# Cross-attention on one core: column parts of 171 in place of 172, another order of work in the first rounds, and two moved shifts in the tail

## The chip, the core and the metric

The kernel runs on one core of a Trainium2 chip. The core has a matrix engine (PE in the profile, with PEld for its weight loads), a vector engine (DVE), a scalar engine (ACT), GpSimd (POOL), and SP, which here only issues DMA transfers. Each engine executes its own list of instructions in order and waits on semaphores for the others. The metric is device time of one execution in microseconds (us), the median of several runs.

## What is computed

Per batch element b (64 of them), with x of 256 x 512 and a context c of 256 x 384, all in fp32:

```python
text_p  = x @ W_text + b_text            # 256 x 512
audio_p = c @ W_audio + b_audio          # 256 x 512
Q = layer_norm(text_p, g1, beta1)
K = layer_norm(audio_p, g2, beta2)
alpha = softmax(Q @ K.T / sqrt(512))     # 256 x 256
h = (alpha @ audio_p) @ W_out + b_out
out = layer_norm(h + x, g_out, beta_out)
```

## The kernel before

**Algebra.** The weights are centred once, so that the layer norms of Q and K need only a mean square. `alpha @ audio_p @ W_out` is computed as `(alpha @ c) @ (W_audio W_out)`; the folded matrix is `wao_sb` (384 x 512), made by `fold_multiply` and `fold_evict` (lines 237 to 249). Two of the three matrix products of a round are done with fewer multiplications than the direct way:

- `Fork` (from line 609), for x times W_text: sums of blocks, seven products in place of eight, on columns of 256. It lives in two PSUM banks, `fork`, with parts R, q1, q2 and q3. `seed` puts a bias row into R, `clear` zeroes q2, then `one`, `seven`, `six`, `five` and `rest` multiply, with `after_one` (copy R to q1, ACT), `after_seven` (copy q2 out, ACT), `after_six` and `after_five` (DVE) between them.
- `Thirds` (from line 502), for c times W_audio (object `k2` of a round) and for z times wao (`old.o`): the 384 inner columns and the 512 output columns are cut in three, 15 products in place of 18. `W3` (line 50) is the width of a column part, 172; the parts start at columns 0, 172 and 340 (`starts`), so that the middle and the last one overlap by four columns. They live in four PSUM banks, `third`, two parts each (M, L, TU, N). `one` to `five` multiply, `after_one`, `after_three` and `after_four` (DVE) combine parts in PSUM between them, `after_five` and `leave`, or `leave_plus` for the output, take the result to rows. `ends(row)` is the first and last part of a row, `middle(row)` the middle one; `room` is a buffer of one or two parts.

Both need sums of blocks of the moving side: `sum_x` (line 289, four additions, on GpSimd except the first) and `Sides` (line 305, seven additions on GpSimd). `third_weights` (line 343) makes the sums of weight parts once, in groups of instructions numbered 0, 3, 1 and 2.

**Order.** `manual_schedule`: each engine executes its instructions in the order of the program text; every line of the main part is therefore a choice of order for each engine that it uses. After the head (lines 975 to 1084) comes the loop `for b in range(B - 2)` (line 1093). Round b multiplies the projections of batch b+2 (`k2`, `q2`), turns the rows of Q and K of batch b+1 (`turn`, a 32 x 32 transposition on DVE of blocks that were stored to DRAM and fetched again by `store` and `fetch`), applies gamma and beta to those of batch b (`affine_keys`, `affine_queries`, ACT), computes the scores of batch b (`at.score`), its maxima (DVE) and exponentials (ACT), the context of batch b-1 (`last.context_one`, `context_two`), and the output of batch b-2 (`old.o`). `settled` is batch b-3, whose final layer norm is done by `shift` (DVE), `scale_row` (ACT) and `lift_rows` (GpSimd), or `settle` (one DVE instruction for the last two of these). Rounds 0, 1 and 2 differ from the others by `if b` cases, because old and last do not exist yet, and because the folded weights are still being made. All DMAs of the loop are issued by SP, in program order: `load_c` and `load_x` (four transfers each), `store`, `fetch`, `store_e`, `fetch_e`.

The tail from line 1295 finishes the last four batches without projections.

Of the kernel before, what the change touches and what calls it, by code (L numbers as in the profile page):

```python
# [9 lines left out]
F32 = mybir.dt.float32  # L10
# [12 lines left out]
def kernel(  # L23
# [25 lines left out]
    scale = 1.0 / math.sqrt(H)  # L49
    W3 = -(-H // 12) * 4  # L50
    starts = (0, W3, H - W3)
# [236 lines left out]

    def sum_x(xT, engine=nc.gpsimd):

        n = DC // 2
        part = lambda i, j: xT[:, j * n : (j + 1) * n, bass.ts(i, P)]
        s = work.tile([P, 4, n, P], F32, tag="xsum", name="xsum")
        add = engine.tensor_tensor
        add(s[:, 0], part(1, 0), part(1, 1), ALU.add)
        add(s[:, 1], s[:, 0], part(0, 0), ALU.subtract)
        add(s[:, 2], part(0, 0), part(1, 0), ALU.subtract)
        add(s[:, 3], part(0, 1), s[:, 1], ALU.subtract)
        ss = {
            1: part(0, 0), 2: part(0, 1), 4: part(1, 1),  # L300
            5: s[:, 0], 6: s[:, 1], 7: s[:, 2], 3: s[:, 3],
        }
        return {p: [ap[:, k, :] for k in range(n)] for p, ap in ss.items()}

    class Sides:
# [37 lines left out]
    def third_weights(w_sb, t, parts=(0, 1), engine=nc.gpsimd):  # L343

        b = [[w_sb[:, c, j : j + W3] for j in starts] for c in range(3)]
        w = {n: t[:, i] for i, n in enumerate((10, 4, 5, 1, 6, 2, 8, 9, 0, 3, 7))}
        w.update({14: b[2][0], 13: b[1][2], 11: b[0][0], 12: b[0][2]})
        plus = lambda o, i0, i1: engine.tensor_tensor(o, i0, i1, ALU.add)
        less = lambda o, i0, i1: engine.tensor_tensor(o, i0, i1, ALU.subtract)
        if 0 in parts:  # L350
            plus(w[0], b[1][1], b[1][2])
            less(w[6], w[0], b[2][0])
            less(w[2], b[1][0], w[0])
            plus(w[0], b[0][0], b[1][0])
            less(w[8], w[2], w[0])
        if 3 in parts:
            plus(w[0], w[0], b[1][2])
            less(w[9], b[1][2], b[2][0])
            less(w[7], b[0][1], b[0][0])
            plus(w[7], w[7], b[0][2])  # L360
        if 1 in parts:
            less(w[3], b[2][1], b[2][0])
            less(w[10], w[3], b[0][2])
            plus(w[4], w[3], b[2][2])
# [137 lines left out]
    class Thirds(Projection):  # L502

        M, L, TU, N = [t[:, : 2 * W3].rearrange("p (n h) -> p n h", n=2) for t in third]
        M0, M1, L0, L1 = M[:, 0], M[:, 1], L[:, 0], L[:, 1]
# [41 lines left out]
        def room(self, tag, n=1):  # L547
            return once.tile([P, n, W3] if n > 1 else [P, W3], F32, tag=tag, name=tag)

# [501 lines left out]
    wa_t = const.tile([P, 11, W3], F32, tag="wa_thirds", name="wa_thirds")  # L1051
# [13 lines left out]
    fold_evict(1)  # L1065
    cT[2] = turn_c(2)
    cs[2] = Sides(cT.pop(2), "csum").add()
    q[1].five()
# [15 lines left out]
    wao_t = wao_room[:, : 11 * W3].rearrange("p (n h) -> p n h", n=11)  # L1084

# [7 lines left out]
    for b in range(B - 2):  # L1093
# [17 lines left out]
        k2.one()  # L1111
        k2.after_one()
        if b < 2:
            Fork.clear()
        if b == 0:
            bias_rest(part, 3, 4)
        if b == 1:
            last.maxima()
        k2.two()
        if old:  # L1120
            old.context_two(0)
            old.context_two(1)
            old.copy_two()
        k2.three()
        if b == 0:
            fold_multiply(2, 2, 4)
            fold_evict(2)
            fold_bias(part)
        if three and b > 1:
            cT[b + 3] = turn_c(b + 3)  # L1130
        if b > 1:
            at.affine_keys(0, 1)
        k2.after_three()
        if b < 2:
            cT[b + 3] = turn_c(b + 3)
        if old:
            old.start_products()
        if b < 3:
            q2.one()
            q2.after_one()  # L1140
        q2.seven()
        q2.after_seven()
        if b > 1:
# [5 lines left out]
        done = settled  # L1149
        if b > 1:  # L1150
            last.fetch_e()
            load_c_rows(b)
            load_x_rows(b - 1)
# [5 lines left out]
        if b == 1:  # L1159
            last.reciprocals()  # L1160
            last.divide_e()
            last.store_e()
            load_c(b + 4)
            last.fetch_e()
            load_c_rows(b)
            load_x(b + 4)
        if b < 2:
            at.q.turn()
            at.k.turn()
            at.affine_keys()  # L1170
        if settled:
            settled.deviations()
        if three:
            cs[b + 3] = Sides(cT.pop(b + 3), "csum").add(2 if b > 1 else 7)
        k2.four()
# [12 lines left out]
        k2.leave()  # L1188
        k2.last_middle()
        if three:  # L1190
            cs[b + 3].add(3 if b > 1 else 0)
        if old:
# [8 lines left out]
        q2.scales()  # L1201
        if b:
            q[b + 1].turn()
            k[b + 1].turn([0])
        if three:
            xT[b + 3] = turn_x(b + 3)
        k2.square()
        if b:
            k2.scales()
            at.score(0, 2)  # L1210
        else:
            at.score(0, 8)
            xs[b + 3] = sum_x(xT.pop(b + 3))
            k2.scales()
        if old:
            old.o.one()
            old.o.after_one()
            old.o.two()
        if b:
            k[b + 1].turn([1])  # L1220
            at.score(2, 4)
# [19 lines left out]
        if old:  # L1241
            old.o.five()
        if three:
            Fork.seed()
            k2.normalise()
            k2.store()
            q2.fetch()
            k2.fetch()
        if three:
# [7 lines left out]
        if b < 2:  # L1257
            wao_blocks = third_weights(wao_sb, wao_t, [[0, 3], [1, 2]][b])
        if b:
            at.maxima()  # L1260
        if three and b:
            Fork.clear()
        if b:
            at.exponentials()
# [44 lines left out]
    settled.shift(0)  # L1309
    settled.shift(1)  # L1310
    old.o.two()
# [3 lines left out]
    old.o.three()  # L1315
    old.o.after_three()
    for t in range(ST):
        last.context_two(t)
# [109 lines left out]
```

## Time and profile before

| | |
|---|---|
| median of 3 runs | 1381.71 us (1380.88 to 1382.01) |
| the profiled execution | 1381.61 us |
| its span, first to last instruction | 1379.8 us |
| mean granted clock of PE in it | 0.999 |
| busy: PE, PEld | 1363.6 us (99%), 1242.3 us (90%) |
| busy: DVE, ACT, POOL | 1102.3 (80%), 1090.2 (79%), 1160.3 us (84%) |
| DMA | 322.02 MB, mean 233 GB/s |

A row of a timeline reads: start in us from the span's start, length in us, engine, line, operation, what it writes `<-` what it reads, partitions x elements, and, in square brackets, how long the engine had been idle before and what ended that. Neighbouring rows of the same kind are merged, with their count after `x`. A row of a group reads: line, engine, operation, tiles, shapes, `x` count, busy us, mean ns of one, idle us before them. Each product of two fp32 matrices appears as two MATMUL records, and the records of consecutive ones overlap: what a product costs is the distance from start to start.

### The profile page before, as it was taken

To read this page: it belongs to the slowest core of one execution; us is meant where nothing else is said; L and a number is where in the kernel's file an instruction comes from. 1 tells how busy PE (TensorE), PEld (TensorE's weight loads), DVE (VectorE), ACT (ScalarE), POOL (GpSimd) and SP (SyncE) were. 2 spreads that over 40 slices of the span, in tenths; PEclk is the share of its full clock that TensorE was granted. 3 is DMA by queue.
4 is the path that set the end of the run, shared out by engine and by line. 5 is a ranking of instruction groups with operands and counts; after the bars stand their busy time and mean duration, and the time that the engine had idled before them with its cause. 6 is when DMAs were issued, how large, how long until landed. Compare 5 with 4: busy or idle time off the path is not lost.

```text
span 1379.8 us, 26390 instructions
## 1 busy us (share of the span) xinstructions
PE 1363.6 (99%) x7423; PEld 1242.3 (90%) x7423; DVE 1102.3 (80%) x2689; ACT 1090.2 (79%) x2688; POOL 1160.3 (84%) x1927
## 2 busy tenths in 40 slices
PE   9899999999999999999999999999999999999997
PEld 4689999999999999999999999999999999999995
DVE  6668888888888878888888888888887888888768
ACT  4578888787887887887888888888888888887884
POOL 5687888888888888888888888888888888888866
PEclk9999999999999999999999999999999999999999
DMA  9599778778788889787888788897888887888673
GB/s 214 161 256 241 241 234 242 230 245 249 234 235 253 232 235 244 232 249 236 244 243 243 238 241 236 238 236 243 246 241 242 236 250 232 237 246 237 206 223 112
DMA packets 449096, 322.02 MB, mean 233 GB/s; under 512 B 153781, under 2 KB 381621, under 8 KB 448950
## 3 DMA queue, kind: packets, MB, share of 16 engines
q1 hardware_dynamic: 448854, 320.20, 80.7%
q8 instruction: 60, 0.98, 0.3%
q14 instruction: 86, 0.70, 0.2%
q10 hardware_dynamic: 96, 0.13, 0.0%
HBM read 203.57 MB, written 116.65 MB: 232 GB/s over the span
## 4 chain that ended last, share of the span: by engine, by line
PE 92%; DVE 2%; DMA 2%; POOL 1%; ACT 1%; issue 1%; SPq 0%; DVEq 0%; POOLq 0%; ACTq 0%
PE ps_f L629 26%; PE ps_m L516 15%; PE ps_sc L697 15%; PE ps_z L763 12%; PE ps_n L516 10%; PE ps_u L516 8%; PE ps_l L516 5%; DMA wt<-in_L_xattn_W_text_dram 1%; POOL csum L327 1%; DMA wo<-in_L_xattn_W_out_dram 1%; DMA c<-in_ctx_dram 0%; ACT qT L491 0%; DMA kd<-kr 0%; PE ps_m L843 0%; DMA cq<-in_ctx_dram 0%
## 5 line engine op out<-in xcount | busy, mean ns | idle before, releaser
L697 PE MATMUL ps_sc<-kT,qT 128*128 128x256 f32 x1024 | 261.5, 379 | 0.0
L327 POOL TENSOR_TENSOR zsum<-zsum,zT 128x256 f32<-128x256 f32 x305 | 193.7, 652 | 14.3
L697 PEld LDWEIGHTS ps_sc<-kT,qT 128*128 128x128 f32 x1024 | 186.2, 190 | 18.2 <-ACT qT L491 1.2
L629 PE MATMUL ps_f<-wtsum,xsum 128*128 128x256 f32 x756 | 184.6, 380 | 2.8 <-ACT ps_f L640 1.6
L763 PE MATMUL ps_z<-eT,c 128*128 128x256 f32 x768 | 186.4, 379 | 0.4 <-ACT e L714 0.3
L327 POOL TENSOR_TENSOR csum<-csum,cT 128x256 f32<-128x256 f32 x310 | 174.4, 571 | 10.0
L763 PEld LDWEIGHTS ps_z<-eT,c 128*128 128x128 f32 x768 | 143.0, 190 | 18.0 <-ACT e L714 0.5
L951 POOL TENSOR_TENSOR yr<-yr,beo 128x512 f32<-128x512 f32 x122 | 153.5, 1280 | 3.6 <-ACT yr L947 3.6
L629 PEld LDWEIGHTS ps_f<-wtsum,xsum 128*128 128x128 f32 x756 | 138.0, 190 | 18.1 <-ACT ps_f L640 2.3
L327 POOL TENSOR_TENSOR zsum<-zT 128x256 f32<-128x256 f32 x122 | 72.4, 593 | 95.3 <-ACT zT L781 95.3
L390 POOL TENSOR_TENSOR rstd<-ve,nhalf 128x2 f32<-128x2 f32 x192 | 136.3, 710 | 16.0
L491 ACT ACTIVATE kT<-kT,columns 128x256 f32<-128x256 f32 x256 | 139.5, 596 | 6.0 <-DVE kT L484 5.1
L491 ACT ACTIVATE qT<-qT,columns 128x256 f32<-128x256 f32 x256 | 139.1, 593 | 2.8 <-DVE qT L75 2.8
L629 PE MATMUL ps_f<-wt,xT 128*128 128x256 f32 x504 | 129.3, 379 | 0.0
L714 ACT ACTIVATE e<-ps_sc,nmx 128x256 f32<-128x256 f32 x128 | 59.5, 470 | 66.5 <-DVE nmx L707 66.5
L933 DVE SCALAR_TENSOR_TENSOR yr<-yr,nm,go 128x512 f32<-128x512 f32 x124 | 103.0, 831 | 0.9 <-ACT junk L826 0.9
L629 PEld LDWEIGHTS ps_f<-wt,xT 128*128 128x128 f32 x504 | 93.1, 190 | 10.7 <-issue 0.7
L500 DVE TENSOR_TENSOR ps_l<-ps_m,t 128x172 f32<-128x172 f32 x248 | 85.8, 346 | 18.3 <-DVE t L557 1.8
L500 DVE TENSOR_TENSOR ps_f<-ps_f,s 128x256 f32<-128x256 f32 x126 | 54.5, 433 | 47.1 <-PE ps_f L629 42.0
L781 ACT COPY zT<-ps_z 128x256 f32<-128x256 f32 x64 | 23.9, 373 | 86.3 <-PE ps_z L763 86.2
L826 ACT ACTIVATE junk<-yr,nm 128x512 f32<-128x512 f32 x124 | 88.0, 713 | 2.8 <-POOL nm L807 2.8
L947 ACT ACTIVATE yr<-yr,rstd 128x512 f32<-128x512 f32 x122 | 87.2, 716 | 1.2 <-POOL rstd L390 1.1
(247 smaller groups left out, 3785.4 us busy)
## 6 DMA issues: line engine op xcount, KB each, us to landing
kd<-kr SPq DMA_DIRECT2D x64, 512.0 KB, 3.1
kq<-kd SPq DMA_DIRECT2D x256, 128.0 KB, 3.1
qd<-qr SPq DMA_DIRECT2D x64, 512.0 KB, 2.8
qq<-qd SPq DMA_DIRECT2D x256, 128.0 KB, 2.7
xq<-in_x_dram SPq DMA_DIRECT2D x252, 128.0 KB, 3.2
x<-in_x_dram SPq DMA_DIRECT2D x63, 512.0 KB, 4.6
out_dram<-yr SPq DMA_DIRECT2D x62, 512.0 KB, 3.9
cq<-in_ctx_dram SPq DMA_DIRECT2D x252, 96.0 KB, 3.2
```

What stands on the lines that cost most here:

```text
L327: nc.gpsimd.tensor_tensor(*step)
L390: nc.gpsimd.tensor_tensor(r, ve, nhalf[:, :n], ALU.pow)
L491: nc.scalar.activation(self.T[:, k, :], self.T[:, k, :], AF.Identity, bias=bet[:, k : k + 1], scale=gam[:, k : k + 1],)
L500: nc.vector.tensor_tensor(o, i0, i1, op)
L516: nc.tensor.matmul(place, lhsT=self.sides.of[n], rhs=self.weights[n], start=(n == 14), stop=True, skip_group_check=True,)
L629: nc.tensor.matmul(place, lhsT=side, rhs=w, start=False, stop=True, skip_group_check=True)
L697: nc.tensor.matmul(self.sc[:, t, :], lhsT=self.q.T[:, k, bass.ts(t, P)], rhs=self.k.T[:, k, :], start=(k == 0), stop=(k == HC - 1),)
L763: nc.tensor.matmul(ps, lhsT=c_rows[self.b][:, s, bass.ts(j, P)], rhs=self.eT[:, s, :], start=(s == 0), stop=(s == ST - 1),)
L826: nc.scalar.activation(junk, self.y[:, t, :], AF.Square, bias=self.nm[:, t : t + 1], accum_out=self.ssq[:, t : t + 1],)
L933: nc.vector.scalar_tensor_tensor(row, row, self.nm[:, t : t + 1], go_sb, ALU.add, ALU.mult)
L947: nc.scalar.mul(self.y[:, t, :], self.y[:, t, :], self.r[t])
L951: nc.gpsimd.tensor_tensor(self.y[:, t, :], self.y[:, t, :], beo_sb, ALU.add)
```

## The change

1. `W3` becomes 171 (`-(-H // 3)`), the parts start at columns 0, 171 and 341 and overlap by one column. Buffers and PSUM parts keep a pitch of `WP` = 172.
2. In the head: `take_columns` (a PE transposition that waits for small vectors from DRAM) stands behind `fold_multiply(0)`; the four additions of the first `sum_x` are spread, s[:, 2] for product 7 first; `turn_c(2)` and its `Sides`, the third group of weight sums, `Thirds.seed_with` and `ba_delta` stand elsewhere. All calls of `sum_x` now do s[:, 2] first.
3. In rounds 0 to 2: other places for `turn`, `affine_keys`, `exponentials`, `divide_e`, `fold_multiply(2, 2, 4)`, `k[2].fetch` and `fetch_e`; in round 1 product `one` of the fork stands before `k2.three`. A group of `third_weights`, [1], is split in [1] and [4].
4. In the tail: `settled.shift(1)` behind `old.o.after_three`, `old.shift(0)` behind `last.o.after_four`; for the last batch, row tile 0 is finished by `scale_row` and `lift_rows` in place of `settle`, and stored last.

No instruction is added to the rounds from 3 on, and none taken away. The diff, cut to its core (the class `SumX` holds the additions of `sum_x` as a list, of which `add(n)` emits the next n):

```diff
-    W3 = -(-H // 12) * 4
+    W3 = -(-H // 3)
+    WP = -(-W3 // 4) * 4
...
-        M, L, TU, N = [t[:, : 2 * W3].rearrange("p (n h) -> p n h", n=2) for t in third]
+        M, L, TU, N = [t[:, : 2 * WP].rearrange("p (n h) -> p n h", n=2)[:, :, :W3] for t in third]
...
-    g1_sb, be1_sb, g2_sb, be2_sb, bac_sb = take_columns()
     turn_weights(2, 2)
...
     xT[1] = turn_x(1)
+    xs_1 = SumX(xT.pop(1), nc.vector)
+    xs_1.add(1)
     k[1].evict(0)
     k[1].evict(1)
     Fork.clear()
+    xs_1.add(2)
...
-    xs[1] = sum_x(xT.pop(1), nc.vector)
-    for v in (g2_sb, be2_sb):
-        nc.vector.tensor_scalar(v, v, scale, None, ALU.mult)
+    xs[1] = xs_1.add()
+    cT[2] = turn_c(2)
...
     k[1].square()
-    ba_delta = third_bias(ba_sb, "ba_delta")
     fold_multiply(0)
+    g1_sb, be1_sb, g2_sb, be2_sb, bac_sb = take_columns()
+    for v in (g2_sb, be2_sb):
+        nc.vector.tensor_scalar(v, v, scale, None, ALU.mult)
...
-    third_weights(wa_sb, wa_t, [1, 2], nc.vector)
+    cs[2] = Sides(cT.pop(2), "csum").add()
+    ba_delta = third_bias(ba_sb, "ba_delta")
+    third_weights(wa_sb, wa_t, [1], nc.vector)
     fold_multiply(1, 0, 2)
     q[1].six()
     q[1].after_six()
+    third_weights(wa_sb, wa_t, [4, 2], nc.vector)
     fold_evict(0)
+    Thirds.seed_with(ba_sb)
...
-    cT[2] = turn_c(2)
-    cs[2] = Sides(cT.pop(2), "csum").add()
     q[1].five()
     q[1].after_five()
     xT[2] = turn_x(2)
...
-    Thirds.seed_with(ba_sb)
...
+            if b == 2:
+                last.fetch_e()
...
         k2.after_one()
+        if b == 0:
+            bias_rest(part, 3, 4)
+            at.q.turn()
         if b < 2:
             Fork.clear()
-        if b == 0:
-            bias_rest(part, 3, 4)
...
         k2.two()
+        if b == 0:
+            fold_multiply(2, 2, 4)
+            fold_evict(2)
+        if b == 1:
+            q2.one()
+            q2.after_one()
...
         k2.three()
         if b == 0:
-            fold_multiply(2, 2, 4)
-            fold_evict(2)
             fold_bias(part)
...
+        if b == 1:
+            last.exponentials()
...
         k2.after_three()
+        if b == 1:
+            last.reciprocals()
         if b < 2:
             cT[b + 3] = turn_c(b + 3)
+        if b == 0:
+            at.k.turn()
...
         q2.after_seven()
-        if b > 1:
+        if b == 1:
+            last.divide_e()
+        if b < 3:
+            at.affine_keys()
+        else:
             at.affine_keys(2, 3)
-        if b == 1:
-            last.exponentials()
...
         if b == 1:
-            last.reciprocals()
-            last.divide_e()
             last.store_e()
+            k[2].fetch()
+            last.fetch_e()
...
-        if b < 2:
-            at.q.turn()
-            at.k.turn()
-            at.affine_keys()
...
-        if b:
-            q[b + 1].turn()
-            k[b + 1].turn([0])
+        q[b + 1].turn()
+        k[b + 1].turn([0])
...
         k2.square()
+        k2.scales()
...
             at.score(0, 8)
             xs[b + 3] = sum_x(xT.pop(b + 3))
-            k2.scales()
...
+        if b == 1:
+            at.maxima()
+            at.exponentials()
...
     settled.shift(0)
-    settled.shift(1)
...
     old.o.after_three()
+    settled.shift(1)
...
     at.shift(0)
-    old.shift(0)
     end.maxima()
     end.exponentials()
     last.o.four()
     last.o.after_four()
+    old.shift(0)
...
     end.evict_halves(1, [0])
+    end.shift(0)
+    end.scale_row(0)
     end.evict_halves(1, [1])
     end.scale_soon(1)
+    end.lift_rows(0, 1)
     end.shift(1)
-    end.shift(0)
-    end.settle(0)
+    end.settle_halves(1)
     end.store(0, 1)
-    end.settle_halves(1)
```

More of the change, by code (lines that the diff above doesn't have):

```diff
@@ L287, in weight_sums, with __init__, add, sum_x @@
         return {p: [ap[:, k, :] for k in range(n)] for p, ap in ws.items()}
[L289 to L303, printed above, removed]
+    class SumX:
+        def __init__(self, xT, engine=nc.gpsimd):
+            n = DC // 2
+            part = lambda i, j: xT[:, j * n : (j + 1) * n, bass.ts(i, P)]
+            s = work.tile([P, 4, n, P], F32, tag="xsum", name="xsum")
+            self.engine = engine
+            self.steps = [
+                (s[:, 2], part(0, 0), part(1, 0), ALU.subtract),
+                (s[:, 0], part(1, 0), part(1, 1), ALU.add),
+                (s[:, 1], s[:, 0], part(0, 0), ALU.subtract),
+                (s[:, 3], part(0, 1), s[:, 1], ALU.subtract),
+            ]
+            ss = {
+                1: part(0, 0), 2: part(0, 1), 4: part(1, 1),
+                5: s[:, 0], 6: s[:, 1], 7: s[:, 2], 3: s[:, 3],
+            }
+            self.of = {p: [ap[:, k, :] for k in range(n)] for p, ap in ss.items()}
+        def add(self, n=4):
+            for step in self.steps[:n]:
+                self.engine.tensor_tensor(*step)
+            self.steps = self.steps[n:]
+            return self.of
+    def sum_x(xT):
+        return SumX(xT).add()
     class Sides:
@@ L345, in third_weights @@
         b = [[w_sb[:, c, j : j + W3] for j in starts] for c in range(3)]
-        w = {n: t[:, i] for i, n in enumerate((10, 4, 5, 1, 6, 2, 8, 9, 0, 3, 7))}
+        w = {n: t[:, i, :W3] for i, n in enumerate((10, 4, 5, 1, 6, 2, 8, 9, 0, 3, 7))}
         w.update({14: b[2][0], 13: b[1][2], 11: b[0][0], 12: b[0][2]})
@@ L363, in third_weights @@
             less(w[10], w[3], b[0][2])
+        if 4 in parts:
             plus(w[4], w[3], b[2][2])
@@ L547, in room @@
         def room(self, tag, n=1):
-            return once.tile([P, n, W3] if n > 1 else [P, W3], F32, tag=tag, name=tag)
+            room = once.tile([P, n, WP] if n > 1 else [P, WP], F32, tag=tag, name=tag)
+            return room[:, :, :W3] if n > 1 else room[:, :W3]
         def after_one(self):
@@ L1050 @@
     q[1].after_seven()
-    wa_t = const.tile([P, 11, W3], F32, tag="wa_thirds", name="wa_thirds")
+    wa_t = const.tile([P, 11, WP], F32, tag="wa_thirds", name="wa_thirds")
     third_weights(wa_sb, wa_t, [0])
@@ L1149 @@
         done = settled
+        if b > 2:
+            last.fetch_e()
         if b > 1:
-            last.fetch_e()
             load_c_rows(b)
@@ L1173 @@
         if three:
-            cs[b + 3] = Sides(cT.pop(b + 3), "csum").add(2 if b > 1 else 7)
+            cs[b + 3] = Sides(cT.pop(b + 3), "csum").add(2 if b else 7)
         k2.four()
@@ L1189 @@
         k2.last_middle()
+        if b == 0:
+            third_weights(wao_sb, wao_t, [1])
         if three:
-            cs[b + 3].add(3 if b > 1 else 0)
+            cs[b + 3].add(3 if b else 0)
         if old:
@@ L1218 @@
             old.o.two()
+        k[b + 1].turn([1])
         if b:
-            k[b + 1].turn([1])
             at.score(2, 4)
@@ L1247 @@
             q2.fetch()
-            k2.fetch()
+            if b:
+                k2.fetch()
         if three:
@@ L1262 @@
             Fork.clear()
-        if b:
+        if b > 1:
             at.exponentials()
```

13 lines of the change are left out of this document (6 added, 7 removed).

## The prediction

> **What bounds the kernel now.** First the page, for the engine that is never idle, then the table by stages.
>
> ```profile
> span 1379.8 us, 26390 instructions
> ...
> PE 1363.6 (99%) x7423; PEld 1242.3 (90%) x7423; DVE 1102.3 (80%) x2689; ACT 1090.2 (79%) x2688; POOL 1160.3 (84%) x1927
> ```
>
> ```profile
> 26.00:106.00 80.00, 73.64 (x343) 58.06 (x344) 52.98 (x115) 52.80 (x130) 61.72 (x109) 1.00 0.78 213
> 106.00:1333.00 1227.00, 1226.90 (x6827) 1140.59 (x6826) 1000.21 (x2462) 1001.39 (x2473) 1060.10 (x1759) 1.00 0.83 240
> 1333.00:1372.00 39.00, 38.73 (x185) 30.79 (x184) 30.83 (x79) 24.64 (x60) 26.28 (x37) 1.00 0.38 122
> 1372.00:1379.80 7.80, 0.23 (x2) 0.00 (x0) 4.13 (x9) 0.09 (x1) 1.72 (x3) 0.74 0.37 134
> ```
>
> The columns are length, then busy time of PE, PEld, DVE, ACT and POOL. From 106 us to 1333 us PE is busy 1226.90 of 1227 us: there only shorter matmuls save time, and the other engines matter only if they come to hold PE up. From 26 to 106 us (the end of the head, and rounds 0 to 2) PE is idle by the record for 6.4 us; behind the last matmul follow 7.6 us of vector work and stores. The timeline of PE shows all waits of that second stage that it counts as idle:
>
> ```profile
> 26.06 0.30 PE L169 MATMUL ps_v<-ident,vectors 128*128 128x128 f32 x1 [0.40 <-DMA vectors<-in_L_xattn_b_audio_dram]
> ...
> 32.73 1.10 PE L629 MATMUL ps_f<-wtsum,xsum 128*128 128x256 f32 x4 [1.25 <-POOL ve L388]
> ...
> 44.52 0.85 PE L516 MATMUL ps_m<-wa,csum 128*128 128x172 f32 x4 [0.54 <-ACT ps_m L530]
> ...
> 47.65 1.10 PE L254 MATMUL ps_bias<-part,ones 128*128 128x512 f32 x2 [0.27 <-DVE part L228]
> ...
> 55.19 0.85 PE L516 MATMUL ps_m<-wa_thirds,cT 128*128 128x172 f32 x4 [0.95 <-DVE ps_u L500]
> ...
> 64.17 0.53 PE L516 MATMUL ps_u<-wa_thirds,csum 128*128 128x172 f32 x2 [0.32 <-DVE ps_u L500]
> ...
> 67.98 1.13 PE L629 MATMUL ps_f<-wtsum,xsum 128*128 128x256 f32 x4 [1.55 <-ACT ps_f L640]
> ...
> 73.03 0.85 PE L516 MATMUL ps_m<-wa_thirds,cT 128*128 128x172 f32 x4 [1.01 <-DVE ps_u L500]
> ...
> 84.09 1.13 PE L763 MATMUL ps_z<-eT,c 128*128 128x256 f32 x4 [0.27 <-ACT e L714]
> ```
>
> These nine add up to 6.6 us. Each costs more than its bracket, because records overlap: the next product should have started about 0.16 us before the previous record ended, and the second record of a product comes about 0.1 us late. So a bracket plus 0.26 is its price, 8.9 us for the nine; with waits too short to leave PE idle I put this pool at about 10 us. The change can win there, in the column width, and in the tail.
>
> **The columns.** What a column costs:
>
> ```profile
> L516 PE MATMUL ps_n<-wa,csum 128*128 128x172 f32 x248 | 46.4, 309 | 0.0
> L763 PE MATMUL ps_z<-eT,c 128*128 128x256 f32 x768 | 186.4, 379 | 0.4 <-ACT e L714 0.3
> L843 PE MATMUL ps_f<-wao,zT 128*128 128x512 f32 x12 | 5.5, 592 | 0.0
> ```
>
> ```profile
> 0.00:1379.80 1379.80, 625.59 (x3720) 585.62 (x3720) 1.00 0.81 233
> ```
>
> A record of 172 columns lasts 309 ns, of 256 columns 379, of 512 columns 592: (379 - 309) / 84 = 0.83 ns a column, and (592 - 379) / 256 = 0.83 again. The second row counts the records of line 516, all of 172 columns: 3720. One column less on each, on an engine that does not stop, is 3720 x 0.83 = **3.1 us**. No row has an odd width or an odd first column (172, 256, 512; starts 0, 172, 340). The bounds are 3.1 us saved, if the line holds, and nothing saved, if an odd width is handled like the next even one; a loss by odd widths has no row either way, and stands as a rival below. I take 3.1, since three widths lie on one line.
>
> **The head, to 40.6 us.** The wait at 26.06 goes: the transposition for the vectors now stands behind eight records of folded products, and its DMA has landed by then.
>
> ```profile
> 27.01 3.60 PE L240 MATMUL ps_m<-wo,waT 128*128 128x512 f32 x8
> ```
>
> They take 3.60 us less the overlap of 0.16, so 3.4, and four of them 1.7. Going earlier only brings PE sooner to the next wait, at 32.73, for product 7. It needs a cleared q2 and the sum s[:, 2], which DVE made third:
>
> ```profile
> 28.51 1.29 DVE L415 TENSOR_TENSOR kr<-ps_f,ba 128x512 f32<-128x512 f32 x2 [1.59 <-DMA kd<-kr]
> 29.93 0.27 DVE L625 MEMSET ps_f<- 128x256 f32 x1
> ...
> 31.81 0.77 DVE L297 TENSOR_TENSOR xsum<-xT 128x256 f32<-128x256 f32 x1
> ...
> 32.98 0.33 DVE L349 TENSOR_TENSOR wa_thirds<-wa 128x172 f32<-128x172 f32 x1
> ...
> 33.60 0.68 DVE L348 TENSOR_TENSOR wa_thirds<-wa_thirds,wa 128x172 f32<-128x172 f32 x1
> ...
> 40.64 1.03 PE L629 MATMUL ps_f<-wt,xsum 128*128 128x256 f32 x4
> ```
>
> Now s[:, 2] fits into the 1.59 us in which DVE waits for a store to land. The memset still ends at 30.2, because that landing is not moved, so product 7 can start at about 30.7, when PE has done the folded products: 2.0 us sooner. Each product of the fork is 1.03 less 0.16, so 0.87 us (last row). Product 7, four folded records and product 6 bring PE to 34.2. But this is partly given back. Seven sums of weight parts ([4, 2]) now stand between `after_six` and `after_five`. Alone one takes 0.33 us, beside GpSimd 0.68, and GpSimd is adding there too (the sums of `cs[2]`, which the change brings forward). `after_six` and the first two weight sums end by about 35.4; seven more take 2.3 to 4.8 us, so `after_five` (some 0.4) ends between 38.1 and 40.6. The products of `rest`, which stood at 40.64, start then, or at 38.5, where PE itself is ready (34.2 + 1.7 + 0.87 + 1.7). The gain at this point is 0 to 2.0 us; I take **0.6**, near the contended end.
>
> **Rounds 0 to 2.** In the order of the rows above:
> - 44.52: the seed of M is copied long before. Bracket plus 0.26: 0.8.
> - 47.65: the bias sum now precedes other DVE work, and 1.7 us of folded products stand between `two` and `three`, which cover `after_one`. 0.5.
> - 55.19: DVE turned Q and K ahead of `after_four`:
>
> ```profile
> 53.27 1.26 DVE L484 STREAM_TRANSPOSE kT<-kq 128x512 f32<-128x512 f32 x2
> 54.46 0.30 DVE L500 TENSOR_TENSOR m<-ps_m,ba_delta 128x172 f32<-128x172 f32 x1
> ```
>
> The turns move ahead of `after_six`, and so the wait of 1.2 goes, but `after_six` now has the turn of K (1.26) and a turn of c before it, so product `five` will wait some 0.4. Net 0.8. ACT also gets gamma and beta done earlier, which takes away two short waits among the scores: 0.3.
> - 64.17: `three` waits for `after_one`, which is two DVE instructions:
>
> ```profile
> 63.31 0.34 DVE L552 COPY n<-ps_n 128x172 f32<-128x172 f32 x1 [3.46 <-PE ps_n L516]
> 63.68 0.35 DVE L500 TENSOR_TENSOR ps_u<-ps_n,n 128x172 f32<-128x172 f32 x1
> ```
>
> `q2.one`, 0.87 us of matmuls, now stands in between and covers them. 0.6.
> - 67.98: the copy of R to q1 stood on ACT behind the scaling of K's rows:
>
> ```profile
> 66.33 1.33 ACT L452 ACTIVATE kr<-kr,rstd 128x512 f32<-128x512 f32 x2 [2.30 <-POOL rstd L390]
> ```
>
> The copy came right behind it. ACT waited 2.30 us, as GpSimd made the four sums of `xs` first. `k2.scales` now precedes those sums. 1.8.
> - 73.03: as 55.19; but `after_six` now stands behind a reciprocal that waits for exponentials, and a turn of c. Of 1.3, 0.5 comes back. 0.8.
> - 80 to 88: exponentials and the division come sooner, so the PSUM buffer of the scores is free for `context_two`: 0.5 at 84.09. SP issues the store of e ahead of the fetch of K's blocks, instead of behind:
>
> ```profile
> 70.95 1.78 SPq L72 DMA_DIRECT2D kq<-kd  x4
> 72.83 0.40 SPq L732 DMA_DIRECT2D ed<-e  x1
> ```
>
> The four K fetches pass behind one store, and wait on nothing new; their turn on DVE comes several us later. If they landed late, `turn`, the turn of e and `context_one` would each move by that. I take 0.3 for earlier e and nothing for K, bounds -0.8 and +0.5.
>
> Sum 6.4, with the head **7.0 us**. The bounds are 3.5, if half of the pool reappears as waits behind what was moved, and 10, the whole pool.
>
> **The tail.** One short wait of PE shows there, and the end of the DVE chain:
>
> ```profile
> 1360.03 0.85 PE L516 MATMUL ps_m<-wao_thirds,zT 128*128 128x172 f32 x4 [0.18 <-DVE ps_u L500]
> ...
> 1375.07 0.75 DVE L942 SCALAR_TENSOR_TENSOR y<-y,rstd,beo 128x512 f32<-128x512 f32 x1
> ```
>
> `old.shift(0)`, moved behind `after_four`, takes that wait away, 0.44 with the overlap, and the other moved shift does the same for a shorter wait. DVE is busy in this stretch as well, so I count 0.4. At the very end `settle(0)`, the second row, leaves DVE (0.75) for ACT and GpSimd, but `shift(0)` now delays the last eviction by about as much as one such instruction, less the time in which DVE waited for PE, and a store of a whole row tile goes last: 0.2. Together **0.6**, bounds 0 and 1.4 (0.44 + 0.75, and 0.2 for the shorter wait).
>
> **Sum.** 3.1 + 7.0 + 0.6 = 10.7 us off the profiled execution's 1381.61 us (span 1379.8 and 1.8 around it), 0.1 below the median of the runs: **1371.0 us**. The bounds with all columns are 1381.6 - 3.1 - 10 - 1.4 = 1367 and 1381.6 - 3.1 - 3.5 = 1375.
>
> **Rivals.**
> 1. *The odd width saves nothing.* PE treats 171 as 172. For it: no odd width in the trace; against it: the line through three widths. 1381.6 - 7.0 - 0.6 = 1374.0 us.
> 2. *The waits come back.* Moved work (the sums of weights ahead of `after_five`, the turns ahead of `after_six`) holds PE elsewhere, and half of the pool stays. For it: DVE beside GpSimd takes twice as long. 1381.6 - 3.1 - 3.5 - 0.6 = 1374.4 us; with rival 1 too, 1377.5.
> 3. *Odd first columns slow DVE until PE waits in each round* (slower). Here is the place:
>
> ```profile
> 123.41 0.52 DVE L500 TENSOR_TENSOR n<-ps_m,x 128x344 f32<-128x344 f32 x1
> 123.84 0.33 DVE L500 TENSOR_TENSOR u<-ps_u,x 128x172 f32<-128x172 f32 x1
> ...
> 124.58 0.33 DVE L599 SCALAR_TENSOR_TENSOR yr<-d,ps_n 128x168 f32<-128x168 f32 x1
> ...
> 124.83 0.51 DVE L599 SCALAR_TENSOR_TENSOR yr<-ps_n,n 128x344 f32<-128x344 f32 x1
> ...
> 126.02 0.75 PE L516 MATMUL ps_n<-wa,csum 128*128 128x172 f32 x4
> ```
>
> The next round's first product overwrites N, which DVE has read by 125.34: 0.68 us of slack, some 0.55 with the handoff. The four DVE rows are instructions with operands at columns 171 or 341, 1.7 us together. Lengthened by a third they eat the slack; from there each 0.1 us costs 60 rounds x 0.1 = 6 us. At 50% more the loss is 0.3 x 60 = 18 us, against 10.7 won: 1389 us. It decides from about 43% on. Against it: no row has a hint of such a cost.
>
> [...]
>
> 4. *The order is not what sets the time*: each gap that closes only moves PE to a landing that has not moved, as that of the store at 28.4. For it: the memset above hangs on one. Against it: none of the eight later brackets is released by a DMA. It would have to meet a width that saves nothing: 1381.6 us.
>
> **How the numbers follow.** Forecast (1367 to 1374) 0.58; rival 1 alone 0.12; rival 2 alone 0.14; both 0.06; rival 3 0.08; no difference 0.02. The range 1367 to 1377 holds the first three, 0.84. About 0.2%, 2.8 us, is what a measurement can tell from no change, so faster means below 1378.9. That takes the forecast, rivals 1 and 2, and half of both: 0.87. Same 0.05, slower 0.08.
>
> **What would show it.** Right: records of line 516 of 308 ns and a period of a full round 0.05 us shorter; no bracket on PE at the transposition of the vectors, at the first `two`, and at `six` of round 1; new, smaller brackets before `rest` in the head and before `five` in rounds 0 and 1, released by DVE. Wrong: line 516 still at 309; brackets on ps_n in every round, released by DVE L599; a wait for a DMA of kq or eq in round 1.

## The result, and the profile after

The changed kernel takes **1371.01 us** (median of 6 runs, 1370.49 to 1372.25) beside 1381.26 us of the kernel before on the same chip (1380.71 to 1382.01): ratio 0.9927, 95% interval [0.9914, 0.994]. The prediction said 1371.0. That the number is met to 0.01 us is luck: by the medians the gain is 10.25 us where 10.7 were forecast, from a start that lay 0.35 us lower (1381.26 where the sum began at 1381.61), and among the terms some were too large, some too small, and one had the wrong sign. The profiled execution took 1370.49 us. It is the shortest of the six runs, and that of the kernel before lay 0.35 us above its median, so the traces show a larger gain than the medians, 11.1 us of span. Its page, then the table by stages (columns as in the prediction):

```profile
span 1368.7 us, 26400 instructions
...
PE 1356.2 (99%) x7423; PEld 1239.6 (91%) x7423; DVE 1112.9 (81%) x2688; ACT 1090.0 (80%) x2689; POOL 1159.8 (85%) x1928
```

```profile
26.00:106.00 80.00, 78.45 (x386) 65.81 (x385) 60.83 (x130) 58.96 (x146) 65.45 (x121) 1.00 0.80 224
106.00:1333.00 1227.00, 1226.77 (x6843) 1140.21 (x6842) 1008.28 (x2467) 1004.03 (x2482) 1060.71 (x1759) 1.00 0.84 240
1333.00:1360.10 27.10, 26.55 (x120) 19.92 (x119) 24.80 (x59) 14.71 (x35) 19.86 (x27) 1.00 0.32 108
1360.10:1368.70 8.60, 0.00 (x0) 0.00 (x0) 4.32 (x8) 0.72 (x1) 3.42 (x4) 0.78 0.34 122
```

Between 26 and 106 us PE is now idle for 1.55 us, where it was 6.4. Behind the last matmul (the last row begins there) stand 8.6 us, where 7.6 stood. The view of PE's waits has only these left beside one at the very start:

```profile
PE ps_f L644 <- DVE ps_f L514: 1.3, 1, 1.3
PE ps_m L858 <- ACT zT L793: 0.5, 1, 0.5
PE ps_f L644 <- ACT ps_f L655: 0.3, 1, 0.3
PE ps_u L530 <- DVE ps_u L514: 0.2, 1, 0.2
```

The columns are us in total, times, longest.

To see where the time went, take one event of each round, the first product of `k2` (its `one`). Its rows on PE's timeline of the kernel before, at the starts of rounds 0 to 3 and of the last one (round 4, at 126.02, stands in the prediction):

```profile
43.23 0.60 PE L516 MATMUL ps_n<-wa,csum 128*128 128x172 f32 x3
62.52 0.60 PE L516 MATMUL ps_n<-wa,csum 128*128 128x172 f32 x3
82.49 0.60 PE L516 MATMUL ps_n<-wa,csum 128*128 128x172 f32 x3
105.11 0.68 PE L516 MATMUL ps_n<-wa,csum 128*128 128x172 f32 x3
1315.02 0.46 PE L516 MATMUL ps_n<-wa,csum 128*128 128x172 f32 x2
```

and of the changed kernel, for rounds 0 to 4 and the last:

```profile
42.14 0.60 PE L530 MATMUL ps_n<-wa,csum 128*128 128x171 f32 x3
58.56 0.74 PE L530 MATMUL ps_n<-wa,csum 128*128 128x171 f32 x4
74.17 0.60 PE L530 MATMUL ps_n<-wa,csum 128*128 128x171 f32 x3
96.42 0.64 PE L530 MATMUL ps_n<-wa,csum 128*128 128x171 f32 x3
117.73 0.45 PE L530 MATMUL ps_n<-wa,csum 128*128 128x171 f32 x2
1303.02 0.45 PE L530 MATMUL ps_n<-wa,csum 128*128 128x171 f32 x2
```

| stretch | before | after | gain | predicted |
|---|---|---|---|---|
| to round 0 | 43.23 | 42.14 | 1.09 | 0.6 |
| round 0 | 19.29 | 16.42 | 2.87 | 2.4 |
| round 1 | 19.97 | 15.61 | 4.36 | 3.2 |
| round 2 | 22.62 | 22.25 | 0.37 | 0.8 |
| round 3 | 20.91 | 21.31 | -0.40 | 0 |
| 57 rounds from round 4 | 1189.00 | 1185.29 | 3.71 | 2.9 |
| then to the end of the last matmul | 57.21 | 57.05 | 0.16 | 0.4 |
| behind it | 7.56 | 8.61 | -1.05 | 0.2 |
| span | 1379.8 | 1368.7 | 11.1 | 10.7 with the columns |

The predicted 3.1 us of columns is put at 60 records a round times 0.83 ns, 0.05 us a round: 2.9 in row six, and 0.2 in the others, which is not added there.

At the end of the tail, PE's last product and the rows behind it:

```profile
1358.61 1.46 PE L911 MATMUL ps_u<-wao,zT 128*128 128x256 f32 x6
...
1359.96 0.75 DVE L948 SCALAR_TENSOR_TENSOR y<-y,nm,go 128x512 f32<-128x512 f32 x1 [0.21 <-ACT junk L841]
1360.63 0.48 DVE L925 SCALAR_TENSOR_TENSOR y<-ps_u,rden,x 128x256 f32<-128x256 f32 x1
...
1363.03 1.25 POOL L966 TENSOR_TENSOR y<-y,beo 128x512 f32<-128x512 f32 x1
1363.09 1.86 DVE L940 SCALAR_TENSOR_TENSOR y<-y,rone,beo 128x256 f32<-128x256 f32 x2 [0.43 <-POOL rone L887]
1364.59 0.83 SPq L943 DMA_DIRECT2D out_dram<-y  x2
1365.51 0.40 SPq L969 DMA_DIRECT2D out_dram<-y  x1
```

The matmul ends at 1360.07, but the eviction of its half starts at 1360.63, behind the shift that the change put there. The last two halves (line 940) take 1.86 us beside GpSimd's addition; before, with GpSimd idle, they took 0.87. And the store of a whole row tile is issued after them, 0.40 us more.

**The theory** from these rows: the columns give 3 us; the order of rounds 0 and 1 gives 7 us; the new end costs 1 us, because DVE and GpSimd work beside each other; and what is left in rounds 2 and 3 depends on transfers. **The rivals**: an odd width saves nothing, and all is order; the tail helps, as predicted; the landings swallow what single steps give.

### The profile page after: what moved, and what is told of

Same layout as the page of the kernel before. It is cut to its first block, busy times and chain, and to the rows that moved or that the text cites. A ratio compares the mean times of both kernels' runs of the same rounds, so it can differ in the third digit from the quotient of the medians.

```text
span 1368.7 us, 26400 instructions
## 1 busy us (share of the span) xinstructions
PE 1356.2 (99%) x7423; PEld 1239.6 (91%) x7423; DVE 1112.9 (81%) x2688; ACT 1090.0 (80%) x2689; POOL 1159.8 (85%) x1928
## 5 line engine op out<-in xcount | busy, mean ns | idle before, releaser
L514 DVE TENSOR_TENSOR ps_l<-ps_m,t 128x171 f32<-128x171 f32 x248 | 85.5, 345 | 17.0
```

What stands on the lines that cost most here:

```text
L514: nc.vector.tensor_tensor(o, i0, i1, op)
```

## The experiments

Kernels that were timed beside each other share the runs of the kernel before. Its median was 1381.26 us beside the changed kernel, 1381.75 beside e1 to e4, 1382.34 beside e5 to e8 and 1381.83 beside e9 to e12, so across these groups the ratios compare better than the times. Single executions of one kernel differ by 1 to 3 us (those of e2 by 5), so effects of that size are read from the traces, larger ones from the medians. There is one trace of each kernel.

**e1: the columns alone.** The kernel before with parts of 171 columns at a pitch of 172.

```diff
-    W3 = -(-H // 12) * 4
+    W3 = -(-H // 3)
+    WP = -(-W3 // 4) * 4
```

> The kernel before with column parts of 171 columns alone; the order of the work is the old one. Theory: an odd width is paid by the column, 3720 matmul records times 0.83 ns, so about 3.1 us less than the kernel before (near 1378.2 us), with the round shorter by 0.05 us and the waits in rounds 0 to 2 all still there. Rival (the odd width saves nothing, and the whole gain is order): 1381.3 us. Rival (odd first columns cost time on VectorE): above 1381.3 us.

1378.74 us (10 runs) against 1381.75 (20 runs), ratio 0.998 [0.9971, 0.9989]: 3.0 us, as the theory has it. Two rows, at rounds 4 and 61, give the period: (1311.99 - 125.83) / 57 = 20.810 us, before (1315.02 - 126.02) / 57 = 20.860.

```profile
125.83 0.60 PE L517 MATMUL ps_n<-wa,csum 128*128 128x171 f32 x3
...
1311.99 0.60 PE L517 MATMUL ps_n<-wa,csum 128*128 128x171 f32 x3
```

That is 0.050 us a round, 60 records times 0.83 ns. The odd width of 171 is paid by the column here. DVE pays a little for odd first columns. The same stretch of 600 us, before and then in e1 (third pair: DVE's busy time):

```profile
400.00:1000.00 600.00, 599.95 (x3340) 557.89 (x3339) 490.08 (x1204) 490.33 (x1212) 521.08 (x866) 1.00 0.83 240
```

```profile
400.00:1000.00 600.00, 599.96 (x3347) 557.74 (x3346) 496.43 (x1212) 491.46 (x1215) 522.75 (x867) 1.00 0.82 241
```

6.35 us more in 29 rounds, 0.22 a round; but e1's stretch also holds eight more instructions. Over the whole span, with 2689 instructions in both, DVE is busy 10.8 us more (1113.1 against 1102.3), 0.17 a round. On the timeline the instructions themselves keep their lengths within some 5 ns; but two of the four with a running sum start 0.11 us after the one before has given up its sum, where they started together with that row before:

```profile
1346.10 0.08 DVE L601 DVE_READ_ACCUMULATOR yr<-d,ps_n 128x1 f32 x1
1346.21 0.51 DVE L601 SCALAR_TENSOR_TENSOR yr<-ps_n,n 128x342 f32<-128x342 f32 x1
```

In the rounds this hides. In e1's tail, whose order is the old one, the stretch to the end of the last matmul is 57.41 us against 57.21, although its 120 records of column parts save 0.1 us.

**e2: the order alone.** The changed kernel with `W3` 172.

> The changed kernel with parts of 172 columns again: order and tail alone. Theory: the 7.2 us of the order and the tail stay, about 1374.1 us, 3.1 us above the changed kernel; the head and rounds 0 to 2 gain about 8, the tail gives 1 back. Rival (the width saves nothing): 1371.0 us.

1375.3 us (5 runs, 1373.38 to 1378.48), ratio 0.9958 [0.9945, 0.9971]; the theory's 1374.1 us lies between its lowest and its second run (1374.91). Width is not without effect, and the order with the tail is worth 6.5 us here. With the 3.0 us of e1 that makes 9.5, where the changed kernel gained 10.25: the two add up within the spread of e2. The wide spread is new. In the profiled execution, the longest of the five, round 3 took 24.7 us in place of 21: DVE waited for K's blocks, and PE for DVE. The rows, then PE's table over the next microseconds (the last three columns: granted clock, DMA share, GB/s):

```profile
111.23 0.71 DVE L498 STREAM_TRANSPOSE kT<-kq 128x512 f32<-128x512 f32 x1 [1.94 <-DMA kq<-kd]
...
113.81 0.53 PE L530 MATMUL ps_u<-wao_thirds,zsum 128*128 128x172 f32 x2 [1.96 <-DVE ps_u L514]
```

```profile
114.00:116.00 2.00, 2.00 (x8) 1.68 (x8) 1.31 (x4) 1.24 (x2) 1.92 (x4) 0.66 0.78 174
116.00:118.00 2.00, 2.00 (x9) 1.91 (x8) 0.00 (x0) 0.00 (x0) 1.92 (x3) 0.50 0.81 210
```

The clock was 0.66 and then 0.50: behind the wait of 1.96 us, some 1.7 us more were lost (0.34 and 0.50 of the two stretches of 2 us).

**e3, e4, e5: the tail.** e3 is the changed kernel with the tail of before, e4 the kernel before with the new tail, e5 the changed kernel with only the end as before:

```diff
     end.evict_halves(1, [0])
-    end.shift(0)
-    end.scale_row(0)
     end.evict_halves(1, [1])
     end.scale_soon(1)
-    end.lift_rows(0, 1)
     end.shift(1)
-    end.settle_halves(1)
+    end.shift(0)
+    end.settle(0)
     end.store(0, 1)
+    end.settle_halves(1)
```

> The changed kernel with the tail of the kernel before. Theory (read from the two traces: the new end costs 1.05 us, the moved shifts bring nothing): from the last matmul's end to the end of the span 7.6 us instead of 8.6, the time about 1370.0 us. Rival (the prediction's sign, the new tail gains 0.6): 1371.6 us, and the difference of the traces lies in the single executions.

> The kernel before with the new tail alone. Theory: about 1.0 us slower than the kernel before, 1382.3 us, all of it behind the last matmul (8.6 us instead of 7.6). Rival (the new tail gains 0.6): 1380.7 us.

> The changed kernel with the end of the tail as before (the second row's finish on VectorE, nothing on GpSimd), the two shifts left where the change puts them. Theory: the loss behind the last matmul (7.6 us before, 8.6 with the new end) is that of the end alone, so 7.6 us here and the time 1.0 us less, about 1370.0 us by the median of the changed kernel. Rival (the moved shifts make the loss): 8.6 us stays.

| kernel | median us | ratio to before | last `one` to the last matmul's end | behind it |
|---|---|---|---|---|
| before | 1381.75 (beside e3 and e4) | | 57.21 | 7.56 |
| e4 | 1382.65 | 1.0008 [0.9999, 1.0017] | 56.89 | 8.60 |
| changed kernel | 1371.01 | 0.9927 [0.9914, 0.994] | 57.05 | 8.61 |
| e3 | 1372.22 | 0.9928 [0.9911, 0.9944] | 57.38 | 7.73 |
| e5 | 1371.84 | 0.9923 [0.9905, 0.994] | 57.05 | 7.74 |

The traces agree: the old end is 0.9 to 1.0 us shorter in every pair, the moved shifts gain 0.32 (172 columns) and 0.33 (171). The medians of e3 and e5 miss what was expected of them by 2 us, so by the time the loss is not shown there. Each of these records has waits behind landings that are as large as the effect (in e3's, PE waits 0.87 us at 112.54, and at 142.50 once more, 0.94); that they account for the 2 us is likely, but not shown. By the time only e4, which lacks the new order, leans the expected way: +0.9 us, with an interval that just includes no change.

**e6: the seven sums of weights behind `after_five`.**

```diff
-    third_weights(wa_sb, wa_t, [4, 2], nc.vector)
...
     q[1].five()
     q[1].after_five()
+    third_weights(wa_sb, wa_t, [4, 2], nc.vector)
```

> The changed kernel with the seven sums of weight parts behind the copy for product five in the head, instead of ahead of it. Theory (the wait ahead of the products of rest, 1.27 us in the changed kernel, comes from these sums): that bracket goes, round 0 starts 1.2 to 1.4 us sooner, and the kernel is about 1.2 us faster, 1369.8 us. Rival (VectorE is full from 35 to 50 us, so the sums hold PE up later): the round starts sooner, but PE waits at product five of round 0 instead, and round 1 starts at the same time, 58.6 us.

1375.26 us, ratio 0.9953 [0.9937, 0.9969], where the changed kernel has 0.9927: about 4 us slower. The wait ahead of `rest` went; the theory that it can be had for nothing fell, and the rival was too mild:

```profile
46.54 0.53 PE L530 MATMUL ps_u<-wa_thirds,csum 128*128 128x171 f32 x2 [1.56 <-DVE ps_u L514]
```

```profile
48.00:49.00 1.00, 1.00 (x3) 0.48 (x2) 0.91 (x4) 0.00 (x0) 0.43 (x1) 0.50 1.03 391
49.00:50.00 1.00, 1.00 (x4) 0.81 (x3) 0.97 (x3) 0.59 (x1) 0.00 (x0) 0.50 0.18 68
```

DVE reaches `after_one` of round 0 late, and PE waits there, with the clock halved behind it. Round 0 takes 20.3 us instead of 16.4.

**e7: two rows of the output fetched early.** `go` and `beo`, 256 KB each, in round 0 and not in round 2.

```diff
-        if b == 2:
+        if b == 0:
             go_sb = row(g_out, "go")
             beo_sb = row(beta_out, "beo")
```

> The changed kernel with the two broadcast rows of the output (gamma and beta, 256 KB each) fetched in round 0, where the DMA engines stand nearly idle for 4 us, instead of round 2. Theory (in round 3 PE waits for VectorE, which waits for K's blocks to land, as the DMA engines still work off what the sooner rounds 0 to 2 left them): the landing of the blocks comes up to 2 us sooner, the wait near 110 us goes (0.2 to 2.1 us in the executions so far), the time is 0.3 to 1.0 us less. Rival (the landing depends on the store and fetch alone): no difference, 1371.0 us.

1369.96 us (4 runs, 1369.51 to 1370.49), ratio 0.9914 [0.9896, 0.9931]. The wait in round 3 is gone, and not in this record alone: round 3 takes 20.8 us in all four records with the early rows (e7 and e10 to e12), and 20.9 to 24.7 in the seven with the new order and the late rows. That ends the rival. The intervals of e7 and of the changed kernel overlap, so the 1 us between the medians is no proof by itself. K's blocks are asked for 4 us sooner: SP fetches Q's blocks, just ahead of them, 2.5 us after the last store was issued (93.77 to 96.30), in the changed kernel 6.3 us after it (94.02 to 100.30), when the landing of the stores allows it (SP waits 5.6 us for that of `qd`). In the changed kernel, SP's row and DVE's:

```profile
102.20 1.89 SPq L73 DMA_DIRECT2D kq<-kd  x4
...
107.56 0.71 DVE L498 STREAM_TRANSPOSE kT<-kq 128x512 f32<-128x512 f32 x1 [0.74 <-DMA kq<-kd]
```

and in e7:

```profile
98.28 1.80 SPq L73 DMA_DIRECT2D kq<-kd  x4
...
106.47 0.67 DVE L498 STREAM_TRANSPOSE kT<-kq 128x512 f32<-128x512 f32 x1
```

**e8: one step undone**, `k2.scales` of round 0 behind GpSimd's four sums again.

```diff
-        k2.scales()
         if b:
+            k2.scales()
             at.score(0, 2)
         else:
             at.score(0, 8)
             xs[b + 3] = sum_x(xT.pop(b + 3))
+            k2.scales()
```

> The changed kernel with one step of the order undone: in round 0 the scales of K's rows are made behind GpSimd's four sums again. Theory (the step's gain is its own, 1.8 us as predicted): round 2 starts 1.3 to 1.8 us later than in the changed kernel (74.2 us) and so does all that follows; 1372.6 us. Rival (the landings in rounds 2 and 3 set the time, and swallow what a step gives): round 2 starts later, but round 4 starts within 0.5 us of the changed kernel's 117.7 us, and the time stays at 1371.0 us.

1375.48 us, ratio 0.9952 [0.9936, 0.9968], about 4 us slower than the changed kernel. The wait comes back as before:

```profile
63.94 1.10 PE L644 MATMUL ps_f<-wtsum,xsum 128*128 128x256 f32 x4 [1.51 <-ACT ps_f L655]
```

Round 1 takes 18.40 us instead of 15.61, 2.8 more; it also holds a wait of 0.40 for the turned e. Round 2 gives 0.6 of it back (21.65 against 22.25). So 2.2 us are left behind the two rounds, more than the 1.8 of the theory, and the rival is out: round 4 starts 4.0 us later, not 0.5. Of these 4.0, 0.5 were there before round 0, and 1.2 came in round 3 (22.55 us against 21.31), where PE waits 0.94 us for DVE, which had waited 1.76 for e's blocks to land. Whether that belongs to the step is not shown: e9, which has the step in place, takes 23.81 us in round 3. Of the single steps of the new order in rounds 0 and 1 only this one was undone.

**e9: the end without GpSimd's last addition.**

```diff
-    end.lift_rows(0, 1)
```

> The changed kernel without the last addition on GpSimd (beta is not added to the first row tile of the last batch, so a part of the output is left out). Theory (the two halves that VectorE finishes last take 1.86 us instead of 0.87 because GpSimd adds beside them): they take 0.9 us again and the end comes about 1 us sooner, 7.6 us behind the last matmul instead of 8.6. Rival (the delay is that of the shift placed ahead of the last eviction, and GpSimd costs nothing): the halves stay near 1.9 us, or the end stays at 8.6.

This kernel leaves beta out of one row tile of the output. It ran once. The two halves take

```profile
1366.40 0.88 DVE L940 SCALAR_TENSOR_TENSOR y<-y,rone,beo 128x256 f32<-128x256 f32 x2 [0.43 <-POOL rone L887]
```

0.88 us again, and the end comes 7.87 us behind the last matmul: the addition beside them is what doubled them, and 0.74 of the 1.05 us. Even so the new end is no gain. The halves start 3.0 us behind the last matmul's end, 0.5 sooner than with the old end (3.5 in e5), but the span ends later than there (7.87 against 7.74), and the store of the whole row tile still goes last.

**e10, e11, e12: towards a faster version.** e10 is e7 with the old end. e11 adds four of the weight sums on GpSimd; e12 also moves the squares of the last batch but two behind the copies of the context.

```diff
-    third_weights(wa_sb, wa_t, [4, 2], nc.vector)
+    third_weights(wa_sb, wa_t, [4], nc.vector)
+    third_weights(wa_sb, wa_t, [2])
```

```diff
-    last.deviations()
     at.evict(1)
     at.scale_soon(1)
     at.shift(1)
     end.context()
+    last.deviations()
```

> The changed kernel with the early fetch of the two rows and the old end of the tail together. Theory (their gains, 1.2 by the medians and 0.9 behind the last matmul, touch different places): 1369.1 us. Rival (the runs with the early rows were only lucky in the landings): 1370.1 us or more.

> The same, and four of the seven sums of weight parts in the head made by GpSimd, which the record shows idle from 40 to 43 us. Theory (VectorE is the bound from 35 to 50 us, so only work taken off it shortens the head): the wait ahead of the products of rest, 1.0 to 1.5 us, goes, and round 1 starts 1.0 to 1.4 us sooner (57.0 us by the changed kernel's record); 1368.0 us. Rival (GpSimd's sums slow VectorE beside them by as much, or K's first sums wait for GpSimd): no difference, 1369.1 us, or more.

> The same again, and in the tail the squares of the last batch but two are summed by ScalarE behind the copies of the last context, not ahead of them. Theory (the products of the output wait 0.68 us for the copy, which stands behind these squares): the last matmul ends 0.6 us sooner, and what follows the squares has slack enough; 1367.4 us. Rival (the squares then delay the statistics of the last rows on ScalarE, and the end moves out by as much): 1368.0 us.

| kernel | median us (runs) | ratio to before |
|---|---|---|
| e10 | 1369.95 (5) | 0.9913 [0.99, 0.9927] |
| e11 | 1368.82 (4) | 0.9906 [0.9893, 0.992] |
| e12 | 1369.06 (4) | 0.9909 [0.9895, 0.9922] |

e10's record has 7.74 us behind the last matmul, so the gain of the end is there, but its median is that of e7: by the time alone this is inconclusive. In e11 the wait ahead of `rest` is gone and round 0 starts at 40.80, but round 1 at 58.59, as in the changed kernel (58.56). The reason, on three engines:

```profile
41.40 2.07 POOL L362 TENSOR_TENSOR wa_thirds<-wa_thirds,wa 128x171 f32<-128x171 f32 x3
...
44.49 1.27 ACT L693 ACTIVATE qr<-ps_f,rstd 128x512 f32<-128x512 f32 x2 [2.81 <-POOL rstd L404]
45.65 0.38 ACT L636 COPY ps_f<-bt 128x256 f32<-128x256 f32 x1
...
46.09 1.13 PE L644 MATMUL ps_f<-wt,xT 128*128 128x256 f32 x4 [1.10 <-ACT ps_f L636]
```

GpSimd's sums stand ahead of the rstd that ACT waits for, and behind that ACT copies the seed for which PE waits: the wait has moved. The rival has the outcome of this step right, though the path is another than the two that it named. The interval of e11 overlaps that of e10, so its lower median is no proof of a gain. In e12 the last matmul ends 0.65 us sooner (56.42 us after the last `one`) and the end comes 8.41 us behind it instead of 7.74: the 0.67 us came back at once, as its rival said: ACT starts the statistics of the last rows 0.20 us ahead of the last matmul's end (1360.20), where it was 1.71 us ahead in e11 (1357.68). The lowest median is that of e11, 1368.8 us, below both kernels, at 0.9906 of the kernel before against 0.9927 for the changed kernel; their intervals overlap.

## Why the prediction was right, and where it was wrong

- **Columns** (3.1): right. e1 measured 3.0 in the time and 0.050 us a round; records of 171 columns last 308 ns. Rival 1 is out.
- **Head** (0.6): the mechanism was right. Product 7 starts at 30.27, and the sums of weights hold `after_five` until `rest` waits:

```profile
36.23 0.77 DVE L361 TENSOR_TENSOR wa_thirds<-wa_thirds,wa 128x171 f32<-128x171 f32 x1
...
37.56 1.49 DVE L362 TENSOR_TENSOR wa_thirds<-wa_thirds,wa 128x171 f32<-128x171 f32 x3
38.97 0.42 DVE L514 TENSOR_TENSOR ps_f<-ps_f,s 128x256 f32<-128x256 f32 x1
...
39.44 1.13 PE L644 MATMUL ps_f<-wt,xsum 128*128 128x256 f32 x4 [1.27 <-DVE ps_f L514]
```

 Forecast were 38.5 to 40.6 for the start of `rest`, it is 39.44. The landing ahead of the memset, which the prediction held fixed, does move: the row behind it starts at 28.51 before, at 27.55 here, and at 26.9 to 29.4 in the eight records with this head. The size of the gain is not shown: round 0 starts at 41.8 to 44.1 us in these eight (mean 42.9), and at 42.5 to 43.4 in three with the old head (mean 43.1); waits at the first loads are part of what varies (DVE waits 3.4 us for `ba` before, 3.1 here).
- **Rounds 0 and 1** (5.6, measured 7.2): all waits of PE above 0.1 us went in this record. The step that failed is the two give-backs ahead of product `five` (0.4 and 0.5): `after_six` was not late. In round 0 it ends at 49.79, and `five` starts at 50.20:

```profile
49.37 0.42 DVE L514 TENSOR_TENSOR ps_f<-ps_f,bt_step 128x256 f32<-128x256 f32 x1
...
50.20 1.03 PE L644 MATMUL ps_f<-wtsum,xsum 128*128 128x256 f32 x4
```

 In round 1 they stand at 63.92 and 64.05. Without the give-backs the prediction's own terms are 2.8 and 3.7, against 2.87 and 4.36. e8 confirms the largest term: predicted 1.8, it costs 2.8 in its round and 2.2 in two. The prediction's sign of being wrong, a wait for the blocks of K in round 1, is there as well: DVE waits 0.18 us for them at 69.13, and 0.33 to 1.64 in the ten other records with the new order. In seven of these PE then waits 0.34 to 1.05 us for the turned e (0.59 at 74.70 in e2). Without e6 and e8, round 1 takes 15.6 to 16.6 us in them and round 2 is shorter when round 1 is longer; both together take 37.9 to 38.3, against 42.59 before. So 4.36 is the best case of round 1, and the wait is mostly made up for in round 2.
- **Rounds 2 and 3** (0.8, measured -0.03): "nothing for K" was taken for the landings of round 1, and round 3 was not looked at. There K's blocks land too late, as PE comes 8 us sooner to the same transfers: 0.2 us of waiting in this record, 2.0 in e2's. e7 removes it. At the end of round 3 e's blocks can be late too: in e5, e8 and e9 DVE waits 1.36 to 1.76 us for them and PE then 0.77 to 0.94 for DVE. In the old order that stands at the end of round 2 (PE waits 0.55 us at 104.97 in e1, 0.82 at 106.14 in e4). Round 2 itself gave 0.37 of its 0.8: product `six` waits 0.28 us at 78.74 for the copy on ACT, a wait that the prediction did not have. Rival 4 is thus partly true, in rounds 1 and 3.
- **57 rounds** (2.9, measured 3.7): the columns give 2.84 of it (e1 takes 1186.16 us for these rounds), and the order 0.9, which the prediction put at nothing: 0.87 between e1 and the changed kernel, 0.91 between the kernel before and e2 (1188.09). In the kernel before and in e1 PE lost about 0.3 us once in 16 rounds (at 245, 579, 912 and 1246 us before), when DVE paused 0.46 us between two instructions; the changed kernel's record has no such wait above 0.12. Chance of one execution it is not: the four losses are in all three records with the old order (e4 too), and of the eleven with the new one in that of e6 alone. Why DVE pauses, and why the order decides whether that costs something, stays open.
- **The tail** (+0.6, measured -0.9): wrong in sign. The moved shifts give 0.33, as forecast (0.4). The term "At the very end ... 0.2" is the step that failed: it counted `settle(0)` as leaving DVE for free, and did not count that DVE's last two instructions then run beside GpSimd, though the prediction used that very doubling in the head. e9 shows it, for 0.74 us. Without the doubling the new end would still be no gain (7.87 us in e9 against 7.74 in e5). One moved shift is longer beside GpSimd as well, 1.57 us, where it and its neighbour took 1.45 together before (at 1342.27, no addition of GpSimd beside them):

```profile
1331.91 2.95 POOL L987 TENSOR_TENSOR x<-x,bao 128x512 f32<-128x512 f32 x2
...
1332.16 1.57 DVE L948 SCALAR_TENSOR_TENSOR yr<-yr,nm,go 128x512 f32<-128x512 f32 x1
```

- **Rival 3** (odd first columns): out as a danger, true as a small effect. In e1 the instructions keep their lengths within some 5 ns; some 0.2 us a round shows, mostly in two late starts of 0.11 us, and the tail lost 0.2 us net, 0.3 without the columns saved there.
- **The range.** Its lower term of 3.5 is half of the 7.0 us counted for the order, and not, as its sentence says, half of the pool of 10. The result lies near the middle either way.

## What to carry to other kernels

PE, which does not stop in these rounds, paid by the column at 171 as at 172 (0.050 us a round, 3.0 us in all in e1), so unneeded overlap between parts is worth removing. When an edit moves work from one engine to another, price it by who works beside it at that place: the addition that looked free on GpSimd doubled DVE's last two instructions (1.86 us beside it, 0.88 without it in e9). And where PE comes sooner to a stage, look at the transfers of the next stages; the wait in round 3 was 0.2 us in the changed kernel's record and 2.0 in e2's.

## What the runs showed of the hardware that was not expected

- The granted clock fell to 0.50 for some 3 to 4 us behind a wait of PE of 1.96 us (e2) and behind one of 1.56 us followed by 0.12 (e6); behind 1.55 us alone (67.98 before, at 1.00 from 66 to 72 us) and 1.82 (47.72 in e12, at 1.00 from 46 to 60 us) it did not. So the length of the wait alone does not decide, and these runs do not show what does.
- Beside GpSimd's additions, DVE's last two instructions took 1.86 us in place of 0.87, and a shift of 128x512 (at 1332.16) 1.57 in place of 0.75; all of these read SBUF alone. One that reads PSUM did not double: an eviction of 128x512 took 0.75 us in the changed kernel, at 1357.52, while GpSimd added beside it, and 0.74 at 1352.35, where it did not. But not all of the first kind doubled: the shift of 128x512 at 102.20, beside GpSimd's sums of 128x256 from 99.96 to 103.30, took 0.79 us. What decides is not shown.
- In e1, whose parts begin at odd columns, two DVE instructions with a running sum start 0.11 us later than before, though no instruction is longer by more than some 5 ns (groups of 510 and 511 ns take 515 and 514).
